# The two first groups of a decoder kernel: from lockstep to leader and follower

## The chip, the cores and the metric

The kernel runs on one core of a Trainium2 chip. A core has five engines that work side by side, each through its own list of instructions in order: PE (TensorE, matmuls and transposes, with PEld for its weight loads), ACT (ScalarE), DVE (VectorE), POOL (GpSimd), and SP (SyncE), which here only issues DMA transfers. They wait for each other through semaphores. The metric is the device time of one execution in microseconds (us); smaller is better. Everything is float32.

## The reference, cut to what matters

There are 32 sequences of 56 tokens with 128 features, and for each sequence a memory of 1500 rows by 128. Two layers follow each other, each with a mixer, a cross attention to the memory and a mixture of experts, and a layer norm after each of the six parts:

```python
x = _layernorm(x + _L0_attn_ref(x, ...))        # 16 heads of 8, window of 32
x = _layernorm(x + _L0_xattn_ref(ctx, ctx, x))  # 1 head of 128, 1500 keys
x = _layernorm(x + _L0_ffn_ref(x, ...))         # 8 experts, 128 -> 512 -> 128, top 2
x = _layernorm(x + _L1_attn_ref(x, ...))        # a gated recurrence along the tokens
x = _layernorm(x + _L1_xattn_ref(x, ctx, ...))  # 16 heads of 64, 1500 keys
x = _layernorm(x + _L1_ffn_ref(x, ...))         # 8 routed experts and a shared one
```

The recurrence is `state = dt * state + (1 - dt) * xt` for 32 state features, with `dt` and `xt` from linear maps of a short convolution; its output is mixed by a gate with another linear map. All experts of both mixtures are computed for all tokens, and weighted.

## The kernel before, in words

The 32 sequences are worked on in 8 groups of 4 (224 tokens, two tiles of 112). A group goes through three stages: *pre* (self attention, first cross attention, first experts, recurrence, and the queries of the second cross attention), *attention* (the second cross attention, which is more than half of the work), and *post* (its projection and the second experts).

Each stage is a Python generator. A `yield` marks a place where the program may put instructions of another generator; a number that is yielded says for how many us of TensorE work the generator should rest, and `None` says that it can't go on yet. There is no other scheduling on the chip: what the generators emit in turn is the order of each engine's list.

In the steady part the generator `attention()` leads, and at each of its yields the loop at the end of the kernel lets `pre(g + 1)` and the `post`s do steps, by a plan in us of TensorE work (`PRE_US`, `share`, `due`). When the attention comes to group g, `pres[g].drain` makes sure that its queries are there.

Before the attention can begin, the queries of group 0 must exist, and there is no attention to hide their computation beside. This opening is the part that the change touches. It computes groups 0 and 1 together, since two groups fill each other's waits. The second group's tiles lie *aside*: in memory that the attention uses later (`s512`, `s384`, `qo[2]` and `m`; the class `Aside`), so that no attention can begin before the second group has left it. Its PSUM banks are those of the attention (`p_s`, three) instead of `p_f` (two). Its first loads of the memory go to `amN`, those of the leader to `cxN`. In the trace a tile of the second group has the name of what it lies in: `s`, `qo`, `m`.

The opening before has three parts, which follow each other:

- `opening_a(0)` and `opening_a(1)`: load, self attention and first cross attention, step by step in turn by `together`. `folding` (a one-time product of the weights of the second cross attention, which needs the 2 MB transfer `heads1`) joins after 10 rounds.
- `opening_b`: `experts_0([first[0], first[1]])` does the experts of both groups in one generator. A weight tile is loaded once and used for both. For expert e it emits the up products and Gelu of group 0, then of group 1, then the down products of expert e-1 for both.
- `opening_c(0)` and `opening_c(1)`: the recurrence of both in turn, and the queries of group 0. `pre(1)`, later, only does the queries of group 1.

The memory is read in loads of 750 KB (`load_x0` for the first cross attention, two sequences at a time; `load_attended` for the second), written back transposed (`memT`), and read again by `load_attended_T` (`amT`). All of them are issued by SP in the order of its list. The first matmul of the attention is the first one that reads `amT`.

The lines of the profile: all matmuls are emitted by the helper at line 142 and transposes at line 151, so their tiles tell them apart. Line 481 is `load_x0`, 1050 `load_attended`, 1053 `load_attended_T`, 507 the store of `memT`, 642 and 644 the experts' weights, 681 the Gelu, 705 the sum over experts, 1165 the load of `heads1`, 319 an affine on ACT, 744 the tanh of the recurrence, 809 the copy of the queries.

Of the kernel before, what the change touches and what calls it, by code (L numbers as in the profile page):

```python
# [9 lines left out]
F32 = mybir.dt.float32  # L10
AF = mybir.ActivationFunctionType
# [53 lines left out]
def decoder_kernel(  # L65
# [241 lines left out]
    def hidden_tile():  # L307
        return mid.tile([P, U0 // D, T], F32, tag="hT", name="hT", bufs=2)
# [271 lines left out]
    def top2(lg):  # L580
        nj = lg.shape[1]

        def col(tag):
            return tiny.tile([TP, nj], F32, tag=tag, name=tag, bufs=2)

        def all_(tag):
            return tiny.tile([TP, nj, E], F32, tag=tag, name=tag, bufs=2)

        def wide_of(c):
            return c.unsqueeze(2).to_broadcast([TP, nj, E])  # L590

        picks = []
        for n in range(2):
            m = col(f"m{n}")
            nc.vector.tensor_reduce(m, lg, AX.X, ALU.max)
            eq = all_("eq")
            nc.vector.tensor_tensor(eq, lg, wide_of(m), ALU.is_equal)
            nc.vector.scalar_tensor_tensor(eq, eq, -float(E), eid_far[:, :nj], ALU.mult, ALU.add)
            first = col("first")
            nc.vector.tensor_reduce(first, eq, AX.X, ALU.min)  # L600
            hot = all_(f"hot{n}")
            nc.vector.tensor_tensor(hot, eid[:, :nj], wide_of(first), ALU.is_equal)
            if n == 0:
# [15 lines left out]
    def router(xT, c0, nj=NJ):  # L619
        ps = bank(p_f, "f")  # L620
        for j in range(nj):
            mm(ps[:TP, j * E : (j + 1) * E], pair(xT, j), sq[:, c0 : c0 + E])
        return ps[:TP, : nj * E].rearrange("p (j e) -> p j e", j=nj)
# [9 lines left out]
        return ps[:TP, :D]  # L633


    def experts_0(groups):

        nu = U0 // D

        def weights(e):  # L640
            wu = wst.tile([P, U0], F32, tag="w0", name="wu0", bufs=4)
            nc.sync.dma_start(wu, wup0[:, e * U0 : (e + 1) * U0])
            wd = wst.tile([P, U0], F32, tag="w0", name="wd0", bufs=4)
            nc.sync.dma_start(wd, wdn0[:, e * U0 : (e + 1) * U0])
            return wu, wd

        def each():
            for k in range(len(groups)):
                place["aside"] = aside if k else None
                yield k  # L650
            place["aside"] = None

        ws = weights(0)
        xT, w, acc, hT = {}, {}, {}, {}
        for k in each():
            xT[k] = to_features(groups[k], "xT")
        yield HOP
        for k in each():
            lg = tiny.tile([TP, NJ, E], F32, tag="lg", name="lg", bufs=2)
            nc.vector.tensor_copy(lg, router(xT[k], C_R0))  # L660
            picks = top2(lg)
            p1 = tiny.tile([TP, NJ], F32, tag="p1", name="p1", bufs=2)
            p2 = tiny.tile([TP, NJ], F32, tag="p2", name="p2", bufs=2)
            nc.vector.tensor_tensor(p2, picks[1][0], picks[0][0], ALU.subtract)
            nc.scalar.activation(p2, p2, AF.Exp)
            nc.vector.tensor_scalar_add(p1, p2, 1.0)
            nc.vector.reciprocal(p1, p1)
            nc.vector.tensor_tensor(p2, p2, p1, ALU.mult)
            w[k] = mix(picks, (p1, p2))
        yield 0  # L670
        for e in range(E + 1):
            last = (ws, dict(hT))
            if e < E:
                if e > 0:
                    ws = nxt
                if e + 1 < E:
                    nxt = weights(e + 1)
                for k in each():
                    hT[k] = hidden_tile()
                    for u in range(nu):  # L680
                        nc.scalar.activation(  # L681
                            hT[k][:, u, :],
                            linear(ws[0][:, u * D : (u + 1) * D], xT[k], T), AF.Gelu,
                            bias=vec[:, C_BUP + e * nu + u : C_BUP + e * nu + u + 1],
                        )
                        if len(groups) == 1:
                            yield 0
                yield 0
            for k in each():
                if e == 0:  # L690

                    wT = work.tile([E, T], F32, tag="wT", name="wT", bufs=1)
                    ps = bank(p_f, "f")
                    for j in range(NJ):
                        mm(pair(ps[:E], j), w[k][:, j, :], ident[:TP, :TP])
                    nc.vector.tensor_copy(wT, ps[:E, :T])
                    if len(groups) == 1:
                        yield HOP
                    acc[k] = [
                        plus(linear(pair(wT, j), bdn, D, TP), groups[k][j], "acc")  # L700
                        for j in range(NJ)
                    ]
                else:
                    for j in range(NJ):
                        nc.vector.scalar_tensor_tensor(  # L705
                            acc[k][j], down(last[1][k], last[0][1], nu, j),
                            w[k][:, j, e - 1 : e], acc[k][j], ALU.mult, ALU.add,
                        )
                        if len(groups) == 1:
                            yield 0  # L710
        both = []
        for k in each():
            both.append([normalize_twice(a, "y") for a in acc[k]])
        yield NORM
        return both


    def recurrent_mixer(both):
        hp = here(hp0, "hp")
        res, hs = [], [h for _, h in both]  # L720
        for t, _ in both:
            r = tok_tile("res")
            nc.vector.scalar_tensor_tensor(r, t, 2.0, rowb("bout1"), ALU.mult, ALU.add)
            res.append(r)
        affine(
            hp[:, :, 1 : S + 1], transposed(hs).rearrange("p (b s) -> p b s", b=G),
            vcol("lnb1"), vcol("lng1"),
# [176 lines left out]

    xin = {}

    def pre(g):
        if g == 1:
            yield from queries_1(query_input(both.pop(1), 1), 1)
            return  # L910
        xs = xin.pop(g) if g in xin else load_x(g)
        if g + 1 < NG:
            xin[g + 1] = load_x(g + 1)
        xs = yield from self_attention(xs)
        xs = yield from cross_attention_0(xs, g)
        (xs,) = yield from experts_0([xs])
        xs = yield from recurrent_mixer(xs)
        xT = query_input(xs, g)
        yield HOP
        yield from queries_1(xT, g)  # L920


    first, both = {}, {}

    def opening_a(g):
        xs = load_x(g)
        load_x0(0, g)
        yield 0
        xs = yield from self_attention(xs)
        first[g] = yield from cross_attention_0(xs, g)  # L930

    def opening_b():
        both[0], both[1] = yield from experts_0([first[0], first[1]])

    def opening_c(g):
        both[g] = yield from recurrent_mixer(both[g])
        if g == 0:
            xT = query_input(both.pop(0), 0)
            yield HOP
            yield from queries_1(xT, 0)  # L940

    attended = set()

# [193 lines left out]
                        if not o.over:  # L1137
                            o.step()

    def together(*threads, lag=0):  # L1140

        n = 0
        while not all(t.over for t in threads):
            for t in threads[:-1] if n < lag else threads:
                if not t.over:
                    t.step()
            n += 1

    flat = sbig.tile([P, CK, 512], F32, tag="s512", name="s512")
    flat = flat.rearrange("p c n -> p (c n)")  # L1150
    room = sbig.tile([P, CK, 384], F32, tag="s384", name="s384")
# [7 lines left out]
    ], folding)  # L1159
    for lo, hi in ((4 * D, 8 * D), (8 * D, N_SQ)):  # L1160
        nc.sync.dma_start(sq[:, lo:hi], sq_w[:, lo:hi])
    starts = [Thread(opening_a(0)), Thread(opening_a(1), aside)]
    for t in starts:
        t.step()
    nc.sync.dma_start(hw, heads1)
    nc.sync.dma_start(w_sh, shared1)
    place["aside"] = aside
    for t, tag in ((qpad0, "qpad"), (hp0, "hp")):
        nc.gpsimd.memset(here(t, tag), 0.0)
    place["aside"] = None  # L1170
    together(*starts, folding, lag=10)
    load_attended_T(0)
    together(Thread(opening_b()))
    together(Thread(opening_c(0)), Thread(opening_c(1), aside))
    pres = [Thread(pre(g)) for g in range(NG)]
    posts = [Thread(post(g)) for g in range(NG)]
    pres[0].over = True
# [121 lines left out]
```

## Time and profile before

| what | us |
|---|---|
| median of three runs | 2385.94 (2383.0 to 2386.28) |
| the profiled execution, its time | 2383.31 |
| the profiled execution, its span | 2381.6 |
| start of the first attention matmul (PE, `s<-qo,amT`) | 276.35 |
| PE busy from 0 to 276 | 202.2, at a mean granted clock of 0.80 |
| PE busy from 276 to 2381 | 2044.9 of 2105, at 0.99 |
| DVE, ACT, POOL busy, share of the span | 60%, 53%, 11% |
| DMA | 163.81 MB, mean 69 GB/s |

The profile is of one execution. Busy time is the time in which an engine has an instruction running; the granted clock is the share of full speed at which TensorE was let run, and a matmul at 0.50 takes about twice as long. A row of the timeline gives the start and length of a run of like instructions, the idle time of the engine before it in square brackets, and what ended that idle time.

### The profile page before, as it was taken

The numbers are of one execution on the slowest core, as the hardware profiler recorded it, in microseconds if no ns is written. First come the engines' busy times: TensorE is split into PE (matmuls) and PEld (weight loads), VectorE is DVE, ScalarE is ACT, GpSimd is POOL, SyncE is SP. The second block draws the span as 40 slices with busy tenths as digits, with TensorE's granted clock in tenths as the row PEclk, the third lists the DMA queues.
The fourth block names the chain that finished last, engine by engine and source line by source line (L and its number), as shares of the span: only waits on it lengthen the run. The fifth ranks groups of instructions, "written<-read, shape, count | busy, mean of one in ns | idle before, by whom it ended". The sixth has DMA issues, their size and how long they took to land. (4 is left out here: it accounts for less than half of the span.)

```text
span 2381.6 us, 37426 instructions
## 1 busy us (share of the span) xinstructions
PE 2247.1 (94%) x14906; PEld 1769.6 (74%) x14906; DVE 1427.0 (60%) x2755; ACT 1262.7 (53%) x2212; POOL 254.3 (11%) x416
## 2 busy tenths in 40 slices
PE   6769799999999999999999999999999999999997
PEld 4548477767876779767887787777787678878787
DVE  3422566766576664766557665666647665566664
ACT  1324365555655456555565556554655555655542
POOL 3100200110021000220003100220002200020000
PEclk8878899999999999999999999999999999999998
DMA  5233010114320233113221133201331022210212
GB/s 157 79 113 91 11 40 26 29 54 122 93 66 16 66 102 108 47 29 108 85 82 37 53 103 94 72 27 59 111 97 58 27 91 62 71 42 28 80 34 82
DMA packets 158159, 163.81 MB, mean 69 GB/s; under 512 B 7417, under 2 KB 134817, under 8 KB 157857
## 3 DMA queue, kind: packets, MB, share of 16 engines
q1 hardware_dynamic: 157984, 161.42, 22.1%
q8 instruction: 118, 1.93, 0.3%
q14 instruction: 57, 0.46, 0.1%
HBM read 135.90 MB, written 25.49 MB: 68 GB/s over the span
## 5 line engine op out<-in xcount | busy, mean ns | idle before, releaser
L142 PE MATMUL v<-amN,s 125*128 125x129 f32 x5376 | 701.3, 276 | 1.8 <-ACT s L1086 1.8
L142 PEld LDWEIGHTS v<-amN,s 125*128 125x128 f32 x5376 | 663.2, 192 | 45.9 <-issue 29.7
L142 PE MATMUL s<-qo,amT 128*125 128x512 f32 (+1 forms) x1536 | 651.5, 547 | 4.7 <-ACT s L998 4.4
L998 ACT COPY s<-s 125x512 f32<-125x512 f32 (+1 forms) x768 | 396.6, 538 | 188.2 <-PE s L142 186.9
L1083 DVE TENSOR_TENSOR s<-s,nb 125x1536 f32<-125x1536 f32 (+1 forms) x256 | 394.3, 1557 | 108.9 <-ACT nb L1075 108.8
L142 PEld LDWEIGHTS s<-qo,amT 128*125 128x125 f32 x1536 | 264.0, 188 | 190.5 <-issue 114.9
L1086 ACT ACTIVATE s<-s 125x1536 f32<-125x1536 f32 (+1 forms) x256 | 337.6, 1327 | 91.3 <-DVE s L1083 87.1
L1001 DVE TENSOR_TENSOR m<-m,s 125x1024 f32<-125x1024 f32 (+1 forms) x256 | 279.0, 1090 | 70.4 <-ACT s L998 65.7
L342 POOL TENSOR_SCALAR rs<-mv 112x1 f32<-112x1 f32 x116 | 46.0, 396 | 1797.9 <-DVE mv L336 1598.8
L1103 ACT ACTIVATE ao<-v,rz 128x128 f32<-128x128 f32 x224 | 80.2, 361 | 176.7 <-DVE rz L1101 174.3
L681 ACT ACTIVATE hT<-f,vec 128x224 f32<-128x224 f32 x224 | 95.3, 449 | 96.8 <-PE f L142 95.1
L142 PE MATMUL f<-xT,wu 128*128 128x224 f32 x448 | 124.2, 381 | 2.8 <-DMA wu<-in_wup_dram 2.0
L142 PE MATMUL f<-pxT,w 128*128 128x224 f32 (+1 forms) x576 | 118.2, 343 | 2.1 <-DMA w<-in_gate_dram 1.3
L1001 DVE TENSOR_TENSOR m<-s 125x1024 f32<-125x1024 f32 x64 | 69.7, 1090 | 83.5 <-ACT s L998 83.2
L142 PEld LDWEIGHTS f<-wd,hT 128*112 128x112 f32 x896 | 104.7, 178 | 13.4 <-ACT hT L681 5.1
L705 DVE SCALAR_TENSOR_TENSOR acc<-f,wmix,acc 112x128 f32<-112x128 f32 x112 | 39.2, 350 | 125.8 <-PE f L142 125.8
L142 PE MATMUL f<-wd,hT 128*112 128x128 f32 x896 | 113.3, 275 | 0.0
L1075 ACT COPY nb<-t 125x512 f32<-125x512 f32 x64 | 34.0, 532 | 148.3 <-PE t L142 148.1
L142 PEld LDWEIGHTS f<-pxT,w 128*128 128x128 f32 x576 | 99.4, 195 | 15.3 <-issue 3.2
L142 PEld LDWEIGHTS f<-xT,wu 128*128 128x128 f32 x448 | 74.0, 194 | 21.2 <-ACT hT L681 7.4
L142 PEld LDWEIGHTS f<-w,h 128*112 128x112 f32 x512 | 67.6, 178 | 24.0 <-issue 9.2
L142 PE MATMUL f<-w,h 128*112 128x128 f32 x512 | 79.7, 279 | 2.0 <-DVE th L870 1.9
(313 smaller groups left out, 2694.2 us busy)
## 6 DMA issues: line engine op xcount, KB each, us to landing
amN<-in_mem_dram SPq DMA_DIRECT2D x36, 750.0 KB
amT<-memT SPq DMA_DIRECT2D x32, 750.0 KB, 4.4
cxN<-in_mem_dram SPq DMA_DIRECT2D x28, 750.0 KB
memT<-big SPq DMA_DIRECT2D x28, 750.0 KB, 5.0
wu<-in_wup_dram SPq DMA_DIRECT2D x56, 256.0 KB, 2.8
wd<-in_wdn_dram SPq DMA_DIRECT2D x56, 256.0 KB, 2.7
w<-in_gate_dram SPq DMA_DIRECT2D x72, 128.0 KB, 2.3
w<-in_up_dram SPq DMA_DIRECT2D x72, 128.0 KB, 2.5
```

The lines of the kernel that those rows point to most:

```text
L142: nc.tensor.matmul(ps, lhsT=lhsT, rhs=rhs, start=start, stop=stop)
L342: nc.gpsimd.tensor_scalar(rs, mv[:, 1:2], mul, add, ALU.mult, ALU.add)
L681: nc.scalar.activation(hT[k][:, u, :], linear(ws[0][:, u * D : (u + 1) * D], xT[k], T), AF.Gelu, bias=vec[:, C_BUP + e * nu + u : C_BUP + ...
L705: nc.vector.scalar_tensor_tensor(acc[k][j], down(last[1][k], last[0][1], nu, j), w[k][:, j, e - 1 : e], acc[k][j], ALU.mult, ALU.add,)
L998: nc.scalar.copy(s[:, c, :], ps[:PK, :n])
L1001: nc.vector.tensor_tensor(m, a, s[:, c - 1 : c + 1, :], ALU.max)
L1075: nc.scalar.copy(nb, ps[:PK, :n])
L1083: nc.vector.tensor_tensor(c, c, nb.unsqueeze(1).to_broadcast([PK, 3, n]), ALU.add)
L1086: nc.scalar.activation(c, c, AF.Exp)
L1103: nc.scalar.activation(o, po[:, :D], AF.Copy, scale=rz)
```

## The change

The opening becomes two generators, `leader` and `follower`, instead of three parts. The leader takes group 0 through everything up to its queries. The follower takes group 1 through the first two stages with a delay of 24 rounds, waits until the leader has emitted its experts (`early["weights"]`), and then does its own experts, with its own loads of all weights. When the leader is over, the follower's sums (`acc`) are copied by POOL out of the aside memory. The rest of group 1, its double normalization, its recurrence and its queries, moves into `pre(1)`, beside the attention of group 0. `experts_0` is a generator for one group again and returns `acc`; the normalization goes to `behind_experts`. The load of `heads1` is issued after the leader's first loads, ahead of the follower's.

```diff
-    def experts_0(groups):
+    def experts_0(xs):
...
-        for k in each():
-            both.append([normalize_twice(a, "y") for a in acc[k]])
-        yield NORM
-        return both
+        return acc
...
     def recurrent_mixer(both):
...
             res.append(r)
+        yield NORM
         affine(
...
+    def behind_experts(acc, g):
+        xs = yield from recurrent_mixer([normalize_twice(a, "y") for a in acc])
+        xT = query_input(xs, g)
+        yield HOP
+        yield from queries_1(xT, g)
+
     def pre(g):
         if g == 1:
-            yield from queries_1(query_input(both.pop(1), 1), 1)
+            yield from behind_experts(early.pop("acc"), 1)
             return
...
-        (xs,) = yield from experts_0([xs])
-        xs = yield from recurrent_mixer(xs)
-        xT = query_input(xs, g)
-        yield HOP
-        yield from queries_1(xT, g)
...
+        acc = yield from experts_0(xs)
+        yield NORM
+        yield from behind_experts(acc, g)
...
-    def opening_a(g):
+    def opening(g):
         xs = load_x(g)
         load_x0(0, g)
         yield 0
         xs = yield from self_attention(xs)
-        first[g] = yield from cross_attention_0(xs, g)
-
-    def opening_b():
-        both[0], both[1] = yield from experts_0([first[0], first[1]])
-
-    def opening_c(g):
-        both[g] = yield from recurrent_mixer(both[g])
+        xs = yield from cross_attention_0(xs, g)
         if g == 0:
-            xT = query_input(both.pop(0), 0)
-            yield HOP
-            yield from queries_1(xT, 0)
+            acc = yield from experts_0(xs)
+            early["weights"] = True
+            yield from behind_experts(acc, g)
+            return
+        while "weights" not in early:
+            yield None
+        acc = yield from experts_0(xs)
+
+        while not leader.over:
+            yield None
+        place["aside"] = None
+        early["acc"] = []
+        for a in acc:
+            t = tok_tile("acc")
+            nc.gpsimd.tensor_copy(t, a)
+            early["acc"].append(t)
...
-    starts = [Thread(opening_a(0)), Thread(opening_a(1), aside)]
-    for t in starts:
-        t.step()
+    leader, follower = Thread(opening(0)), Thread(opening(1), aside)
+    leader.step()
     nc.sync.dma_start(hw, heads1)
     nc.sync.dma_start(w_sh, shared1)
...
-    together(*starts, folding, lag=10)
+    n = 0
+    while not (leader.over and follower.over):
+        for t, at in ((leader, 0), (folding, 10), (follower, 24)):
+            if n >= at and not t.over:
+                t.step()
+        n += 1
     load_attended_T(0)
-    together(Thread(opening_b()))
-    together(Thread(opening_c(0)), Thread(opening_c(1), aside))
```

More of the change, by code (lines that the diff above doesn't have):

```diff
@@ L645, in weights @@
             return wu, wd
[L647 to L651, printed above, removed]
         ws = weights(0)
-        xT, w, acc, hT = {}, {}, {}, {}
-        for k in each():
-            xT[k] = to_features(groups[k], "xT")
+        xT = to_features(xs, "xT")
         yield HOP
[L658 to L669, printed above, removed]
+        lg = tiny.tile([TP, NJ, E], F32, tag="lg", name="lg", bufs=2)
+        nc.vector.tensor_copy(lg, router(xT, C_R0))
+        picks = top2(lg)
+        p1 = tiny.tile([TP, NJ], F32, tag="p1", name="p1", bufs=2)
+        p2 = tiny.tile([TP, NJ], F32, tag="p2", name="p2", bufs=2)
+        nc.vector.tensor_tensor(p2, picks[1][0], picks[0][0], ALU.subtract)
+        nc.scalar.activation(p2, p2, AF.Exp)
+        nc.vector.tensor_scalar_add(p1, p2, 1.0)
+        nc.vector.reciprocal(p1, p1)
+        nc.vector.tensor_tensor(p2, p2, p1, ALU.mult)
+        w = mix(picks, (p1, p2))
         yield 0
+        acc = []
+        hT = None
         for e in range(E + 1):
-            last = (ws, dict(hT))
+            last = (ws, hT)
             if e < E:
@@ L677, in experts_0 @@
                     nxt = weights(e + 1)
[L678 to L697, printed above, removed]
-                        yield HOP
[L699 to L710, printed above, removed]
@@ L711, in experts_0 @@
-        both = []
-        for k in each():
-            both.append([normalize_twice(a, "y") for a in acc[k]])
-        yield NORM
-        return both
+                hT = hidden_tile()
+                for u in range(nu):
+                    nc.scalar.activation(
+                        hT[:, u, :], linear(ws[0][:, u * D : (u + 1) * D], xT, T), AF.Gelu,
+                        bias=vec[:, C_BUP + e * nu + u : C_BUP + e * nu + u + 1],
+                    )
+                    yield 0
+            if e == 0:
+                wT = work.tile([E, T], F32, tag="wT", name="wT", bufs=1)
+                ps = bank(p_f, "f")
+                for j in range(NJ):
+                    mm(pair(ps[:E], j), w[:, j, :], ident[:TP, :TP])
+                nc.vector.tensor_copy(wT, ps[:E, :T])
+                yield HOP
+                for j in range(NJ):
+                    acc.append(plus(linear(pair(wT, j), bdn, D, TP), xs[j], "acc"))
+            else:
+                for j in range(NJ):
+                    nc.vector.scalar_tensor_tensor(
+                        acc[j], down(last[1], last[0][1], nu, j),
+                        w[:, j, e - 1 : e], acc[j], ALU.mult, ALU.add,
+                    )
+                    yield 0
@@ L905, in decoder_kernel @@
     xin = {}
+    def behind_experts(acc, g):
+        xs = yield from recurrent_mixer([normalize_twice(a, "y") for a in acc])
+        xT = query_input(xs, g)
+        yield HOP
+        yield from queries_1(xT, g)
     def pre(g):
         if g == 1:
-            yield from queries_1(query_input(both.pop(1), 1), 1)
+            yield from behind_experts(early.pop("acc"), 1)
             return
@@ L915, in pre @@
         xs = yield from cross_attention_0(xs, g)
-        (xs,) = yield from experts_0([xs])
-        xs = yield from recurrent_mixer(xs)
-        xT = query_input(xs, g)
-        yield HOP
-        yield from queries_1(xT, g)
-    first, both = {}, {}
-    def opening_a(g):
+        acc = yield from experts_0(xs)
+        yield NORM
+        yield from behind_experts(acc, g)
+    early = {}
+    def opening(g):
         xs = load_x(g)
@@ L929, in opening_a @@
         xs = yield from self_attention(xs)
-        first[g] = yield from cross_attention_0(xs, g)
-    def opening_b():
-        both[0], both[1] = yield from experts_0([first[0], first[1]])
-    def opening_c(g):
-        both[g] = yield from recurrent_mixer(both[g])
-        if g == 0:
-            xT = query_input(both.pop(0), 0)
-            yield HOP
-            yield from queries_1(xT, 0)
+        xs = yield from cross_attention_0(xs, g)
+        if g == 0:
+            acc = yield from experts_0(xs)
[13 more added lines that the diff above has]
+            early["acc"].append(t)
     attended = set()
@@ L1138, in drain @@
                             o.step()
[L1140 to L1145, printed above, removed]
-                    t.step()
-            n += 1
     flat = sbig.tile([P, CK, 512], F32, tag="s512", name="s512")
@@ L1161, in decoder_kernel @@
         nc.sync.dma_start(sq[:, lo:hi], sq_w[:, lo:hi])
-    starts = [Thread(opening_a(0)), Thread(opening_a(1), aside)]
-    for t in starts:
-        t.step()
+    leader, follower = Thread(opening(0)), Thread(opening(1), aside)
+    leader.step()
     nc.sync.dma_start(hw, heads1)
```

## The prediction

> **What bounds the kernel now.** I read the table of windows first, then the timelines of PE and SP over the first 300 us. Windows (length, busy us of PE, PEld, DVE, ACT and POOL with instruction counts, granted clock, DMA share, GB/s):
>
> ```profile
> 0.00:59.00 59.00, 38.98 (x246) 25.70 (x246) 19.35 (x35) 11.41 (x22) 18.54 (x49) 0.83 0.53 159
> 112.00:148.00 36.00, 17.51 (x70) 10.84 (x67) 3.84 (x8) 5.46 (x10) 0.00 (x0) 0.62 0.47 148
> 200.00:243.00 43.00, 43.00 (x319) 41.54 (x319) 9.74 (x29) 18.76 (x48) 1.13 (x4) 1.00 0.24 75
> 243.00:276.00 33.00, 17.57 (x64) 11.48 (x63) 19.34 (x69) 7.21 (x17) 13.48 (x35) 0.69 0.03 8
> 276.00:440.00 164.00, 161.22 (x929) 121.38 (x928) 105.76 (x126) 100.67 (x169) 0.00 (x0) 1.00 0.11 34
> 276.00:2381.00 2105.00, 2044.94 (x13577) 1614.21 (x13575) 1330.31 (x2479) 1177.73 (x2034) 206.19 (x302) 0.99 0.21 65
> ```
>
> From 276 on PE is busy 97% of the time: work added there costs its PE time. Before 276 PE is busy 202 of 276 us: only there can waits be saved. The waits are at 0 to 59 (loads), 112 to 148 (loads of the memory) and 243 to 276 (chains through DVE and POOL). The joint experts, 200 to 243, have none.
>
> PE's timeline (start, length, idle before, releaser):
>
> ```profile
> 45.85 2.07 PE L142 MATMUL v<-s 64*128 64x128 f32 x8 [3.05 <-DMA s<-in_heads_dram]
> ...
> 86.82 1.25 PE L151 MATMUL f<-ident,cxN 125*128 125x125 f32 x5
> ...
> 119.88 2.88 PE L151 MATMUL f<-ident,cxN 125*128 125x125 f32 x12 [6.53 <-DMA cxN<-in_mem_dram]
> 127.73 2.89 PE L151 MATMUL f<-ident,cxN 125*128 125x125 f32 x12 [4.97 <-DMA cxN<-in_mem_dram]
> ...
> 143.68 2.73 PE L151 MATMUL s<-ident,amN 125*128 125x125 f32 x12 [3.42 <-DMA amN<-in_mem_dram]
> ...
> 199.79 0.99 PE L142 MATMUL f<-xT,wu 128*128 128x224 f32 x4 [2.01 <-DMA wu<-in_wup_dram]
> ...
> 269.39 7.13 PE L142 MATMUL f<-xT,m 128*128 128x224 f32 x24 [0.63 <-ACT xT L319]
> 276.35 1.02 PE L142 MATMUL s<-qo,amT 128*125 128x512 f32 x2
> ```
>
> SP's timeline:
>
> ```profile
> 20.57 7.87 SPq L481 DMA_DIRECT2D amN<-in_mem_dram  x2
> 28.48 8.00 SPq L1165 DMA_DIRECT2D s<-in_heads_dram  x1
> ...
> 109.53 7.02 SPq L481 DMA_DIRECT2D cxN<-in_mem_dram  x2
> 116.64 15.40 SPq L481 DMA_DIRECT2D amN<-in_mem_dram  x2
> ...
> 163.50 6.81 SPq L481 DMA_DIRECT2D cxN<-in_mem_dram  x2
> 170.41 16.28 SPq L1050 DMA_DIRECT2D amN<-in_mem_dram  x2
> ```
>
> Memory loads follow each other at 8 us each (119.88, 127.73, 143.68 for the first, second and fourth of those issued from 109.53). What SP lists behind a pair waits 16 us for it.
>
> **The change, part by part.** The sum goes from event to event, by the changed program's own lists for PE and SP (an order, no times), with lengths from the rows above.
>
> *Start.* The 2 MB for the folding move ahead of the follower's two loads: 16 us earlier, so they land at 45.85 - 16 = 30. The leader reaches its first folding matmul at about 22 (its scores start at 12.48 and 15.03, then four rounds of DVE, POOL and ACT at 0.6, 0.93 and 0.58 us), so PE waits 8 us there. From the folding to the first transposes of `cxN` took 86.82 - 45.85 = 41 us with two groups. One group with the same folding: bounds 27 (two thirds) and 41; I take 32, nearer the lower end since the second group's half of the DVE, POOL and PE work is gone but the folding stays. Event: 62.
>
> *Leader's first pair.* From 86.82 to the end of its values at 109.4 are 22.6 us, beside the follower's like work. Now the follower's self attention lies beside it, on the same engines: 23. Event: 85. The second pair's loads take 127.73 - 109.53 = 18: 103. The follower's rest of self attention, some 6 us of PE, fills part of it.
>
> *Leader's second pair* from its last landing to its values took 163.4 - 143.68 = 19.7; with the follower's 24 transposes in the list 20.5. Event: 123.5.
>
> *The follower's second pair.* SP now lists the leader's loads for group 2 (two) ahead of these two. Four loads took 143.68 - 109.53 = 34: they land at 157.5. PE has the leader's first expert before that, and then its list blocks: the transposes of `amN` stand ahead of the next experts' matmuls. I count some 17 us lost here. From there to the follower's values the list holds, besides the cross attention that took 19.7, eight up and eight down pairs of the leader's experts; about 24 (bounds 20 and 28). Event: 181.5.
>
> *Two attention loads* come next on SP, ahead of the up weights of the leader's sixth expert. Four loads before them took 199.79 - 163.5 = 36; two take 20: 201.5. PE's list has about 10 us of work until then, so 10 more are lost.
>
> *Leader's last three experts.* One expert for both groups takes 213.12 - 206.49 = 6.63 us at full clock (starts of the up rows), 3.31 for one group; at clock 0.5 twice that. Alone, with two PSUM banks, an up product waits for the Gelu (449 ns each): I take 4.2, the first at half clock, plus the last down products (1.9): 17 (bounds 12 and 21). Event: 218.5.
>
> *Leader's tail.* From the experts' end (243.2) to the first query matmul (269.39) are 26 us with two groups in turn on DVE and POOL. One group, with the follower's experts between its steps: 19 (bounds 14 and 26). Queries: from 269.39 to 278.9 less two attention matmuls of 0.85 each makes 7.8; with the follower's up and down products between, 10.5. Event: 248.
>
> *Follower's end.* The lists leave it four up and five and a half down products of experts: 4.3 experts at 3.65 (three banks) and a last down of 1.75, about 17 (bounds 14 and 28, the latter at half clock). The attention starts at **266**.
>
> Before, it starts at 276.35 with 1.7 us of queries still to come, so 278 in effect: 12 us gained.
>
> *Beside the attention.* The recurrence of group 1 leaves the opening. Its ten PE rows at 252.03 to 261.9 hold 9 us for two groups, partly at half clock; about 3 for one at full clock, transposes included. PE idles 2.8 of 164 us there. Bounds 0 (it fits in that idle time) and 9 (its whole stretch in the opening); I take 3, as the list lets other work stand between. The two POOL copies of 112x128: POOL's like row (`res`) has 0.43 us each; POOL is idle in that stretch. If they stood on the path, 1 us.
>
> *Edits with no price of their own.* Sixteen more weight loads of 256 KB: they land in 2.8 us, while DMA share is 0.24 in the expert stretch; each is issued about one expert (3.65 us) ahead of its use, and an expert shorter than about 3.2 would wait for it. Four more table loads on ACT before the attention (1.28 each in ACT's row); PE has matmuls beside two, the pair before the follower's second exponentials is in the 24 above. One `NORM` rest more for groups 2 to 7 adds no instruction; those threads run beside a PE that is 97% busy, so between -2 and +2.
>
> *Sum:* 2383.3 (the profiled execution) - 12 + 3 = 2374.3. That execution stands 2.6 under the median of the three runs, so **2377**.
>
> **A rule against the trace.** The rows are PE's windows:
>
> ```profile
> 184.20:187.60 3.40, 3.40 (x12) 2.15 (x10) 0.96 (x3) 0.69 (x2) 0.00 (x0) 0.50 0.36 96
> 187.60:191.00 3.40, 3.40 (x11) 2.83 (x11) 0.58 (x2) 1.14 (x3) 0.00 (x0) 0.50 0.37 96
> 191.00:194.40 3.40, 3.40 (x13) 3.12 (x12) 0.00 (x0) 2.00 (x5) 0.00 (x0) 0.50 0.37 96
> 194.40:197.80 3.40, 3.38 (x29) 3.17 (x28) 1.05 (x3) 0.00 (x0) 0.00 (x0) 0.95 0.75 185
> ```
>
> PE is busy without a gap and stays at half clock for 10 us. The Trainium skill ("TensorE: Matmul & The Clock Gate", Part 1: The HAM clock gate) says that one busy window of about 3.4 us lifts the throttle, and that an idle window brings it back. By that rule each of the change's four long waits (at 22, 95, 140 and 192) would cost some 1.7 us of slow matmuls, an estimate from the page, and the sum would be 2370. By the row each costs about 5, as the events above have it. Either way the rule speaks against the change: it adds waits in which PE goes cold and breaks up the one stretch at full clock.
>
> **Rivals.**
> - *The staggering hides more.* If the follower's work fills the waits at 95, 140 and 192 (20 us of the 35 counted), the attention starts at 256: 2367. For it: 202 of 276 us is all the PE work there is. Against: the lists are in order, and the blocking transposes stand ahead of the experts.
> - *Slower: half clock from 201 to the end of the opening.* The leader's three experts cost 6.6 instead of 4.2 (+5 with the first already so), the follower's 4.3 experts +12.5, the tail +3: the attention starts at 286, 2397. For it: 174 to 195 and 246 to 273 were mostly at 0.50 with the same kinds of work. Against: 195 to 246 stayed at full clock. It decides the sign when the opening loses 9 us, that is when the attention starts after 275.
> - *Nothing left.* The opening gains 8, and the recurrence with its stretched chain costs 8 beside the attention: 2386.
>
> **How the numbers follow.** Measurement tells a change from none at about 0.2%, 4.8 us. The forecast's case (the start between 258 and 270) is 2369 to 2381 and has 0.45; the hidden waits 0.13; nothing left (2381 to 2391) 0.19; slower 0.23. Faster is 0.13 and 0.43 of the forecast's 0.45: 0.56; the same 0.2 and slower 0.24. The range leaves out 0.1 on either side: 2363 (start at 252) to 2398 (the half clock rival).
>
> **What would show it.** First `s<-qo,amT` matmul near 266. PE waiting at 22 for `s<-in_heads_dram`, at 140 to 157 for `amN`, at 192 to 201 for `wu`. 64 loads each of `wu` and `wd`. From the first attention matmul to group 2's first transposes (446.94 - 276.35 = 170.6 now) about 3 us more. Wrong would be: a first attention matmul after 275, a granted clock near 0.5 from 200 on, or over 6 us added to that distance.

## The result

The changed kernel takes 2389.29 us, the kernel before 2384.21 (medians of 15 runs each); the ratio is 1.0024, with a 95% interval of 1.0016 to 1.0033. It is slower by a quarter of a per cent, where 2377 and a gain were forecast. The profiled execution after has a span of 2387.8 us, 6.2 more than that of before.

The windows of the changed kernel, with the columns of the prediction's table of windows:

```profile
0.00:59.00 59.00, 42.80 (x265) 30.40 (x266) 19.65 (x36) 11.71 (x22) 18.50 (x48) 1.00 0.55 159
112.00:148.00 36.00, 22.36 (x182) 15.00 (x182) 13.67 (x46) 16.44 (x28) 1.48 (x4) 0.87 0.34 107
185.00:200.00 15.00, 2.38 (x21) 2.29 (x21) 3.50 (x17) 0.45 (x1) 0.05 (x1) 0.76 0.54 138
200.00:243.00 43.00, 35.09 (x178) 26.73 (x179) 15.02 (x53) 16.92 (x36) 6.68 (x18) 0.82 0.24 74
243.00:276.00 33.00, 32.84 (x183) 25.99 (x182) 11.98 (x32) 15.12 (x36) 3.50 (x10) 0.98 0.29 92
276.00:2387.00 2111.00, 2044.80 (x13566) 1617.11 (x13564) 1330.18 (x2496) 1171.55 (x2028) 192.97 (x314) 0.99 0.21 65
```

The stretch from 243 to 276, half idle before, is full now, and a hole stands at 185 to 200.

The clock of 1.00 in the first row is not a measurement of full clock. The clock records of this execution begin at 56.4 us (of the one before: at 30.9), and the view counts the time ahead of the first record as full. The length of like matmuls shows that TensorE was slow there. The last 40 matmuls of the folding, in the changed kernel and then in e1_no_rest, a later run whose lists are the same up to the attention (shortest, median and longest in ns, then the first and last start):

```profile
L142 PE MATMUL v<-s x40: 417/417/579, 37.6 to 51.9; 64*128 64x128 f32 x40
```

```profile
L142 PE MATMUL v<-s x40: 272/272/432, 37.6 to 46.4; 64*128 64x128 f32 x40
```

In the kernel before, the same matmuls take 417 ns at a recorded clock of 0.50 and 272 ns at 1.00. So this execution ran at half clock up to 56.4, where e1_no_rest was at full clock from 37.8 on. For the same reason the clocks given so far for the windows of the kernel before that start at 0 (0.80 and 0.83) are too high.

PE's timeline shows the events of the forecast one by one:

```profile
29.58 4.92 PE L142 MATMUL v<-s 64*128 64x128 f32 x24 [5.72 <-DMA s<-in_heads_dram]
...
67.29 1.04 PE L151 MATMUL f<-ident,cxN 125*128 125x125 f32 x4
...
105.12 1.90 PE L151 MATMUL f<-ident,cxN 125*128 125x125 f32 x8 [4.58 <-DMA cxN<-in_mem_dram]
...
148.90 1.09 PE L151 MATMUL s<-ident,amN 125*128 125x125 f32 x4 [13.39 <-DMA amN<-in_mem_dram]
...
157.09 0.65 PE L151 MATMUL s<-ident,amN 125*128 125x125 f32 x2 [4.25 <-DMA amN<-in_mem_dram]
...
201.14 3.54 PE L142 MATMUL f<-xT,wu 128*128 128x224 f32 x8 [13.28 <-DMA wu<-in_wup_dram]
...
242.57 2.45 PE L142 MATMUL f<-xT,m 128*128 128x224 f32 x8
...
267.94 8.75 PE L142 MATMUL s<-qo,amT 128*125 128x512 f32 x20
```

(In the changed kernel's lines, 641 and 643 load the experts' weights, 1041 is `load_attended`, and 345 is the last step of a normalization, on DVE.)

The attention starts at 267.94, for which 266 were forecast. So the opening did gain, and the loss is behind it. The start of the first attention matmul of each fourth sequence cuts the trace into groups:

| | opening | group 0 | groups 1 to 6 |
|---|---|---|---|
| before | 278.0 | 167.2 | 1683.9 |
| after | 267.9 | 175.4 | 1691.8 |
| difference | -10.1 | +8.2 | +8.0 |

(For the kernel before, the 1.7 us of queries that stand behind its first two attention matmuls are counted as opening; its first attention matmul starts at 276.35.) The differences, taken before rounding, add up to +6.1. Group 7 and the end are alike in both.

Group 0, the kernel before and then the kernel after (busy us of PE, PEld, DVE, ACT and POOL, then the granted clock):

```profile
278.00:445.20 167.20, 164.42 (x967) 125.08 (x966) 109.93 (x131) 103.41 (x171) 0.00 (x0) 1.00 0.11 33
```

```profile
267.90:443.40 175.50, 170.46 (x985) 127.52 (x984) 117.55 (x162) 105.37 (x175) 9.79 (x22) 0.99 0.11 34
```

PE is 6.0 us longer busy and 2.3 us longer idle (5.0 for 2.8). One window of half clock of 3.4 us, at 302, is new there; it can account for 1.7 of the 6.0. That leaves some 4.3 of work, an estimate.

The last 20 us before group 2's attention, before and then after:

```profile
706.70:726.70 20.00, 19.34 (x132) 17.51 (x131) 13.81 (x26) 11.04 (x23) 1.56 (x2) 1.00 0.12 39
```

```profile
707.70:727.70 20.00, 18.43 (x115) 18.12 (x116) 11.34 (x24) 8.86 (x17) 3.67 (x7) 0.83 0.03 12
```

and PE's waits in that place after, for the normalized rows of the next group's queries:

```profile
705.82 0.32 PE L151 MATMUL f<-ident,h 112*128 112x112 f32 x1 [0.53 <-DVE h L345]
...
709.27 0.45 PE L151 MATMUL f<-ident,h 112*128 112x112 f32 x1 [2.22 <-DVE h L345]
```

The same two transposes stood at 698.75 and 700.44 before, 28 and 26 us ahead of the next group's attention; now they stand 22 and 18 us ahead. The windows before groups 3, 5, 6 and 7 are alike: PE 17.8 of 20 us at a clock of 0.91, against 19.3 at 1.00. Before group 4 PE is busy for 17.3 us at full clock, so the idle time comes without a window of half clock too. What the change does to the pre stage of groups 2 to 7 is one more `NORM`, a rest of 6 us of TensorE work, between the experts' sums and the double normalization; besides, it drops some empty yields in the experts and moves the `NORM` that was there behind the next step.

A sentence ahead of the prediction has to be corrected. It says that what the generators emit in turn is the order of each engine's list. That is not so everywhere. SP issues the tokens of groups 2 and 3 (`xin`, four loads) at 39 us before and at 45 us after, though the generators emit them long after the opening's first steps; some step behind the generators draws instructions forward. The prediction itself went by the lists after that step.

### The profile page after: what moved, and what is told of

Read it like the earlier page. It is cut to its first block, busy times and chain, and to the rows that moved or that the text cites. A ratio compares the mean times of both kernels' runs of the same rounds, so it can differ in the third digit from the quotient of the medians.

```text
span 2387.8 us, 37452 instructions
## 1 busy us (share of the span) xinstructions
PE 2251.3 (94%) x14906; PEld 1766.2 (74%) x14906; DVE 1425.9 (60%) x2755; ACT 1267.3 (53%) x2216; POOL 236.8 (10%) x418
## 5 line engine op out<-in xcount | busy, mean ns | idle before, releaser
L342 POOL TENSOR_SCALAR rs<-mv 112x1 f32<-112x1 f32 x124 | 35.4, 286 | 1646.4 <-DVE mv L336 1490.2
L142 PE MATMUL f<-xT,wu 128*128 128x224 f32 x448 | 125.6, 382 | 14.2 <-DMA wu<-in_wup_dram 13.3
```

The source lines that it names most:

```text
L142: nc.tensor.matmul(ps, lhsT=lhsT, rhs=rhs, start=start, stop=stop)
L342: nc.gpsimd.tensor_scalar(rs, mv[:, 1:2], mul, add, ALU.mult, ALU.add)
```

## The experiments

All ratios are to runs of the kernel before on the same chip. Stretches are of one profiled execution each. *Fourth sequences* is the sum, over groups 1 to 6, of the last sequence's stretch, in which the next group's queries are finished; it varies least between executions.

| kernel | opening | group 0 | groups 1 to 6 | fourth sequences | median | ratio (95%) |
|---|---|---|---|---|---|---|
| before | 278.0 | 167.2 | 1683.9 | 342.5 | 2384.21 | 1 |
| changed | 267.9 | 175.4 | 1691.8 | 351.3 | 2389.29 | 1.0024 (1.0016 to 1.0033) |
| e1_no_rest | 262.7 | 175.5 | 1683.6 | 344.1 | 2379.26 | 0.9999 (0.9987 to 1.001) |
| e2_before_rest | 277.5 | 167.2 | 1684.9 | 349.1 | 2388.53 | 1.0032 (1.0021 to 1.0043) |
| e3_rec_in_opening | 281.3 | 169.9 | 1687.0 | 351.8 | 2393.11 | 1.006 (1.0048 to 1.0072) |
| e5_rec_alone | 272.1 | 175.0 | 1688.0 | 344.3 | 2385.55 | 1.0021 (1.0013 to 1.003) |
| e6_late_load | 258.9 | 175.6 | 1686.1 | 344.5 | 2372.74 | 0.9959 (0.9943 to 0.9975) |
| e7_later_rec | 266.4 | 173.9 | 1681.6 | 344.3 | 2374.4 | 0.9961 (0.9948 to 0.9975) |
| e8_all | 252.0 | 180.2 | 1679.6 | 344.1 | 2364.99 | 0.9927 (0.9912 to 0.9942) |
| e9_loads_apart | 248.7 | 174.0 | 1678.9 | 343.0 | 2359.47 | 0.9923 (0.9906 to 0.9939) |
| e10_rest_early | 266.2 | 176.7 | 1719.8 | 338.5 | 2416.66 | 1.0161 (1.0142 to 1.018) |

(For before, e2_before_rest and e5_rec_alone the opening includes the 1.7 us of queries behind the first attention matmuls.)

The openings differ by some us also where nothing in them was changed, and this difference arises early: with the same lists, the changed kernel has its second pair of memory loads at 105.1 and e1_no_rest at 98.6. From this second landing (the second wait for `cxN`) to the start of the attention it is 162.8 us in the changed kernel, 164.1 in e1_no_rest, 163.0 in e7_later_rec and e10_rest_early, 159.0 in e6_late_load, 148.6 in e8_all and 148.1 in e9_loads_apart. For what a change does to the rest of the opening these distances are the better measure.

### The rest, taken out and put in

```diff
         acc = yield from experts_0(xs)
-        yield NORM
         yield from behind_experts(acc, g)
```

> The changed kernel without the added rest between the experts' sums and the double normalization of groups 2 to 7 (one line); nothing else. Theory (the rest makes each group's queries late, and the last steps before the next group stand with too little attention beside them): the stretches of groups 1 to 6 fall back by 8 us in all to those of the kernel before (281.2, 283.2, 279.1, 280.7, 279.1, 280.6), the total to about 2381, ratio to the kernel before 0.9985 to 0.999. Rival (the longer groups come from the other order of tiles and loads that the change leaves behind, not from the rest): the stretches stay at 284.0, 283.4, 281.8, 282.3, 280.4, 280.0 and the total at 2389. Group 0 stays at 175 in both.

The stretches of groups 1 to 6 fall from 1691.8 to 1683.6, which is what the kernel before has, and group 0 stays at 175.5. The ratio falls from 1.0024 to 0.9999. The 0.999 that was expected at most was not reached, though its interval holds it: without the rest the change is neither faster nor slower, as far as can be measured. (The profiled execution is the fastest of its eleven, 5 us under their median, so its stretches are a low measure, the opening's 262.7 above all.) The same stretch before group 2, in this kernel:

```profile
699.30:719.30 20.00, 19.58 (x135) 17.81 (x134) 13.99 (x26) 11.28 (x24) 1.32 (x2) 1.00 0.12 39
```

The other way round, the rest alone in the kernel before:

```diff
         # experts_0, ahead of the normalization
+        if len(groups) == 1:
+            yield NORM
         both = []
```

> The kernel before with only this rest put in, at the same place, for groups 2 to 7. Theory of the rest: the fourth sequence of each group takes 1 to 2.6 us longer, 8 us in all, ratio 1.003; a window of half clock appears near the end of most groups. Rival (order of tiles and loads): no change, ratio 1.000.

The median is 8 us above the kernel before, 1.0032, as expected, and the fourth sequences take 349.1 for 342.5. In the profiled execution, the second fastest of its six, other sequences were shorter, so that the sum over groups 1 to 6 shows only 1.0 us of it: these sums move by some us from one execution to the next. The place looks like that of the changed kernel:

```profile
707.10:727.10 20.00, 17.77 (x121) 17.22 (x121) 12.60 (x28) 8.92 (x17) 4.95 (x8) 0.91 0.08 33
```

So the rest costs about 8 us by itself here, and taking it out of the changed kernel gave 6 by the ratios. Is it that the last steps come late, or the rest at any place?

```diff
-            work_.append((pres[group + 1], PRE_US, p / 0.88))
+            work_.append((pres[group + 1], PRE_US, p / 0.82))
```

> The changed kernel with its rest kept, but the plan for the pre stage ends earlier (due by p / 0.82 instead of p / 0.88). Theory (the rest costs only because it makes the last steps late, with too little attention left beside them): the last 20 us of each group are as before (PE 19.3 busy, full clock), the fourth sequences at 57 to 58, groups 1 to 6 sum to 1684, total 2381, ratio 1.000. Rival (a rest between sums and normalization costs by itself, at whatever place): 1690 or more in all, total 2389, ratio 1.002 to 1.003.

Half of the theory holds: with the whole pre stage drawn forward the fourth sequences take 338.5, less than in the kernel before, and the last 20 us are full, at full clock:

```profile
707.70:727.70 20.00, 19.40 (x114) 16.43 (x115) 14.66 (x25) 11.36 (x23) 5.36 (x3) 1.00 0.20 61
```

The total was missed by far. The earlier steps now crowd the other sequences (the second one of a group takes 71 to 74.5 for 67 to 68), and groups 1 to 6 take 28 us more. So the hole at the group's end goes when the steps come earlier, which fits lateness. But the edit moves the whole pre stage, not the rest alone, and leaves less of it to the fourth sequences; that the price of the rest is lateness and nothing else is not shown by it. The total of the rival, 1690 or more, isn't ruled out either. The plan's 0.88 is not free to move.

### The recurrence, in the opening or beside the attention

The changed kernel with group 1's normalization and recurrence in the follower's part of the opening:

```diff
         acc = yield from experts_0(xs)
-        while not leader.over:
-            yield None
-        ...
+        early["both"] = yield from recurrent_mixer([normalize_twice(a, "y") for a in acc])
```

> The changed kernel, rest kept, with group 1's normalization and recurrence put back into the follower's part of the opening; beside the attention only its queries stay. Theory (the recurrence costs 7 to 8 us beside the first attention, more than the 3 forecast, through waits and half clock in its first sequences): group 0's stretch falls from 175.4 to 167 to 169, the first attention matmul comes later by the follower's own chain, 15 to 20 us (it stands alone at the end), so the total is 8 to 13 us above the changed kernel, 2397 to 2402. Rival (group 0 is longer because the attention starts with the follower's leftovers, not because of the recurrence): group 0 stays at 173 to 175, total 2404 to 2410.

Group 0 falls to 169.9, so 5.5 of its 8.2 us go with the recurrence and its normalization, and the rival's 173 is not what came; the other 2.7 us are not accounted for. The start moves from 267.9 to 281.3, since the chain stands alone at the end of the opening, and the ratio is 1.006, 8.6 us above the changed kernel: as expected. In the staggered opening the recurrence is therefore better beside the attention. PE's waits at the end of that opening (in this kernel, 715 and 757 are steps of the recurrence on DVE):

```profile
269.67 0.32 PE L151 MATMUL s<-ident,s 112*128 112x112 f32 x1 [1.68 <-DVE s L345]
272.24 0.45 PE L151 MATMUL s<-ident,s 112*128 112x112 f32 x1 [2.25 <-DVE s L345]
274.72 3.79 PE L142 MATMUL s<-qo,sq 128*32 128x224 f32 x10 [2.03 <-DVE qo L715]
...
280.80 0.66 PE L142 MATMUL s<-sq,qo 128*112 128x128 f32 x4 [1.63 <-DVE qo L757]
```

The same move alone, in the kernel before, with its lockstep:

```diff
-        both = []
-        for k in each():
-            both.append([normalize_twice(a, "y") for a in acc[k]])
+        both = [[normalize_twice(a, "y") for a in acc[0]]]
+        ...                      # acc[1] is copied out by POOL
...
+            pair_ = [normalize_twice(a, "y") for a in both.pop(1)]
+            yield NORM
+            xs = yield from recurrent_mixer(pair_)
...
-    together(Thread(opening_c(0)), Thread(opening_c(1), aside))
+    together(Thread(opening_c(0)))
```

> The kernel before, in lockstep, with only one part of the change: group 1's sums are copied out by POOL and its normalization, recurrence and queries go beside the attention of group 0. Theory: the opening loses the second thread of the last chains, 276 to about 269; group 0 gains 6 to 8 us as in the changed kernel; total within 3 us of the kernel before. Rival (PE price alone, 3 us): group 0 at 172, total 4 us below the kernel before, 2380.

The first attention matmul comes at 270.4 instead of 276.35; with the queries behind it the opening falls from 278.0 to 272.1, and group 0 rises from 167.2 to 175.0. The ratio is 1.0021: a loss of some 5 us, more than the 3 us that the theory allowed, and far from the rival's gain. In lockstep the second thread in the last chains cost 5.9 us, and the same work beside the attention 7.8. The other 4 us of this execution, the slowest of its eleven, lie in groups 1 to 6, where nothing was changed.

Is it the place, the first blocks, in which the products with the values do not run yet?

```diff
         if g == 1:
+            yield 45.0
             yield from behind_experts(early.pop("acc"), 1)
```

> The changed kernel without the rest, and with group 1's normalization, recurrence and queries held back by 45 us of TensorE work, past the first sequence of the attention. Theory (the recurrence is dear because it falls into the first blocks, where the matmuls on the values do not yet run and little stands beside it): group 0's stretch falls from 175.5 to 171 to 172, total 2375, ratio 0.998. Rival (its chain costs the same at any place beside the attention): the 7 us move from the first sequence to the second, stretch 175, total 2379.

The first sequence takes 26.8 us instead of 33.9, but the third 57.4 instead of 50.8; group 0 falls by 1.6 only. The rival is nearer: the chain takes 6 to 7 us at either place. The theory of the place falls for most of the price. The ratio is 0.9961, 9 us below e1_no_rest's (6 us by the medians, each against the kernel before on its own chip), of which the profiled stretches of the two show 1.6 in group 0 and 2.0 in groups 1 to 6; since the profiled execution of e1_no_rest lies 5 us under its median, little of that is settled.

### The waits of the opening

The two waits of 13 us, at 135 and at 187, were forecast from SP's list. SP's timeline of the changed kernel:

```profile
87.07 6.71 SPq L481 DMA_DIRECT2D cxN<-in_mem_dram  x2
...
122.90 6.66 SPq L481 DMA_DIRECT2D cxN<-in_mem_dram  x2
133.95 11.06 SPq L481 DMA_DIRECT2D amN<-in_mem_dram  x2
...
178.61 0.79 SPq L1041 DMA_DIRECT2D amN<-in_mem_dram  x1
...
186.02 0.78 SPq L1041 DMA_DIRECT2D amN<-in_mem_dram  x1
186.90 8.63 SPq L641 DMA_DIRECT2D wu<-in_wup_dram  x1
```

The two `cxN` loads at 122.90 are for group 2, needed some 300 us later. They were held back by a data dependence, a small POOL write into the tile that reads the follower's sums, behind the opening:

```diff
-            elif max(g + 1, 2) < NG:
-                load_x0(0, max(g + 1, 2))
+            elif g and g + 1 < NG:
+                load_x0(0, g + 1)
...
+    for i in range(2):
+        nc.gpsimd.tensor_copy(cxN[i][:1, 0, :1], early["acc"][1][:1, :1])
+    load_x0(0, 2)
     load_attended_T(0)
```

> The changed kernel without the rest, and the leader's loads of the memory for group 2 made to wait for the end of the follower's experts (a small POOL write into the tile that reads them), so that they no longer stand ahead of the follower's second pair and of the weights. Theory (the two waits of 13 us in the opening are the queue of 8 us loads): the follower's second pair lands 16 us earlier, the first attention matmul comes at 248 to 252 instead of 263 to 268, total 2365, ratio to the kernel before 0.993 to 0.995. Rival (PE finds no work for that time, or the half clock takes it): start at 260 or later, total 2376 or more.

The ratio is 0.9959, 9.5 us better than e1_no_rest's, but the start is 258.9, where 248 to 252 were expected. The first wait falls from 13.4 to 9.0 us only, because the follower's own loads, which can't start before its first pair is done (at 128.6 here, at 134.0 in the changed kernel), still take 16; the second stays:

```profile
139.13 1.10 PE L151 MATMUL s<-ident,amN 125*128 125x125 f32 x4 [8.97 <-DMA amN<-in_mem_dram]
...
192.07 3.55 PE L142 MATMUL f<-xT,wu 128*128 128x224 f32 x8 [13.48 <-DMA wu<-in_wup_dram]
```

So the two loads for group 2 held up the opening by 4 to 5 us, which is also what the distances from the second landing show (159.0 for 162.8 to 164.1). The rest of the 9.5 lies elsewhere and is not settled by one profiled execution of each.

With e7's rest of 45 us added, and the load for the second attention sequence held back in the same way:

```diff
+    nc.gpsimd.tensor_copy(amN[1][:1, 0, :1], early["acc"][1][:1, :1])
```

> Both of the former, and the load of the second attention sequence also held back behind the follower's experts. Theory: start of the attention at 240 to 245, since the weights of the leader's sixth expert then wait for one load of 8 us instead of two; group 0's stretch 171 to 172; total 2354 to 2358, ratio 0.989 to 0.991. Rival (loads that are held back collide with the first loads of the attention): group 0's stretch over 176, total 2362 or more.

The second wait falls from 13.5 to 5.0 us, the distance from the second landing to the start from 159.0 to 148.6, and the ratio is 0.9927. The start is 252.0 where 240 to 245 were expected. The rival's collision is there too: the three loads that are held back now stand ahead of the second load of the transposed memory, and group 0 takes 180.2:

```profile
283.44 2.04 PE L142 MATMUL s<-qo,amT 128*125 128x512 f32 x2 [4.18 <-DMA amT<-memT]
```

So the loads for group 2 were made to wait for group 1's normalized rows instead, inside the stretch of group 0 (the lines that held them back in the opening go, the one for `amN` stays):

```diff
             yield from behind_experts(early.pop("acc"), 1)
+            for i in range(2):
+                nc.gpsimd.tensor_copy(cxN[i][:1, 0, :1], res1[1][1][:1, :1])
+            load_x0(0, 2)
```

> As the last kernel with everything together, but the loads of the memory for group 2 wait for group 1's normalized rows beside the attention (about 395), instead of standing ahead of the second load of the transposed memory at 254. Theory (the 4.2 us wait of PE for that load, the half clock after it and the slower first sequence are the collision): the start stays at 250 to 254, group 0's stretch falls from 180.2 to 173 to 175, total 2359, ratio 0.990. Rival (the first sequence is longer for another reason): group 0 stays near 180, total 2365.

The loads are issued at 327, not at the 395 that was expected. Group 0 is back at 174.0, so the collision was the reason. The start is 248.7; the 3.3 us against e8_all lie ahead of the second landing, and this profiled execution is the fastest of its six. The median is 2359.47, the ratio 0.9923 (0.9906 to 0.9939). This kernel is faster than both: the leader and follower, without the rest, with the 45 us of e7_later_rec and with three loads moved. Its interval overlaps that of e8_all, so the last step by itself is shown in the stretch and not in the ratio.

## Why the prediction was wrong

The likeliest case, and the sign, were wrong; the opening was right nearly event by event. In the profiled executions a gain of 9 us was forecast and a loss of 6.1 measured. Of these 15 us, 1.9 lie in the opening, 5.2 in the recurrence beside the attention, and 8.0 in a term that was put at nothing, the rest.

- *Start to follower's end.* The forecast's events against the measured ones: folding 30 and 29.6, first `cxN` transposes 62 and 67.3, second landing 103 and 105.1, the follower's second pair landed 157.5 and 157.1, the up weights 201.5 and 201.1, first attention matmul 266 and 267.9. The waits of 17 us for `amN` and 10 us for `wu` measured 13.4 + 4.3 and 13.3. The forecast's gain of 12 measured 10.1. Reading the lists of SP and PE against the 8 us of a memory load was enough for that. It is not exact to more than some 5 us, and that it came within 2 is partly luck: the first `cxN` transposes came 5 us late, with half clock up to 56.4, and the leader's first pair, from 67.3 to the issue of the next loads at 87.07, took 19.8 us where 23 were forecast. e1_no_rest has the same lists up to there, was at full clock from 37.8, and starts at 262.7.
- *Beside the attention.* The step was "I take 3, as the list lets other work stand between". It measured 8.2: about 4.3 of PE work, up to 1.7 for a window of half clock and 2.3 of idle PE. The ends of the range, 0 and 9, held it; the value was taken from the wrong end. The row of the kernel before that was nearest, 9 us for the whole stretch of two groups in the opening, was set aside with the words above. e5_rec_alone and e7_later_rec show 7.8 and 6.7 us for it. One of the prediction's own signs of being wrong came with it: from the first attention matmul to group 2's first transposes, at 445.10, it is 177.2 us, 6.6 more than the 170.6 of before.
- *Edits with no price of their own.* This is the step that failed outright: "One `NORM` rest more for groups 2 to 7 adds no instruction; those threads run beside a PE that is 97% busy, so between -2 and +2". It measured 8.0 in the stretches, and e1_no_rest and e2_before_rest give 6 and 8 us of it in the medians, taken out and put in. That the rest costs this much is shown by these two runs; how it does so is read from the traces: a rest adds no work, but it moves the same work towards a due time, the next group's attention (the transposes for its queries stood 22 and 18 us ahead instead of 28 and 26), where less is left to stand beside it. PE was idle 2.2 of the last 20 us instead of 0.7 in most groups, and went to half clock for a window. The plan lets the pre stage end near 0.88 of the group; what stands behind it had not been read in the windows of before.
- *The rival "slower"* named half clock from 201 to the end of the opening. That did not happen: the opening ended at 268, at a clock of 0.82 and 0.98 in the last two windows. The rival "nothing left" had the right size for the second step (8 us beside the attention) and lacked the rest; that its 2386 came nearest to 2389 is partly luck.
- *The rule on the clock.* The Trainium skill ("TensorE: Matmul & The Clock Gate", Part 1: The HAM clock gate) would lift the half clock after one busy window of 3.4 us; the prediction stayed with a row that showed 10 us. After the wait for the weights, half clock held on until 210.0, about 9 us after PE had resumed at 201.14. But PE was not busy all that time, it waited 2.1 us for a Gelu ahead of 206.79. The recorded stretches of half clock in this opening last 3.4, 6.8, 13.7 or 17.1 us, so windows of 3.4 us that end at 210.0 fit them:

```profile
203.10:206.50 3.40, 1.59 (x4) 0.78 (x4) 0.88 (x6) 3.34 (x5) 0.00 (x0) 0.50 0.19 61
206.60:210.00 3.40, 3.21 (x15) 3.21 (x16) 0.35 (x1) 0.47 (x2) 0.00 (x0) 0.50 0.03 11
210.00:213.40 3.40, 3.34 (x19) 2.17 (x19) 0.35 (x1) 1.79 (x4) 0.00 (x0) 1.00 0.25 77
```

  The first window in which PE was nearly always busy is the last one at half clock, which is what the rule gives. So this wait agrees with the page, the prediction's row (10 us without a gap at 0.50) does not, and no run here settles what makes the difference. The prediction's 2370 by the page was also not carried through: four waits at 3.3 us less each would be 13 us, not 7.

## What to carry to other kernels

A rest or a yield in a plan with due times is work moved, not nothing: before it is priced at zero, read the window in front of the due time and ask what is left there to stand beside the moved steps. A chain of small dependent steps beside a full engine costs more than its instructions on that engine; here 7 to 8 us for some 4 of matmuls, at any of the places tried. In an opening that loads set, SP's list and the time of one load forecast the events to some 5 us, and a load that nobody needs yet can be taken out of the way with a data dependence, but whatever it then stands in front of has to be looked up as well.

## What was not expected of the hardware

- Memory loads, in packets of 512 bytes, ran at about 8 us for 750 KB, some 96 GB/s, in the stretches looked at, while the 2 MB of `heads1`, in packets of 16 KB, landed within about 7 us of the end of the loads ahead of it (316 GB/s from 23.0 to 29.6). That the size of the packets is the reason was not tested. The order on SP mattered more than the number of bytes: the 16 extra weight loads of the change (4.2 MB) caused no wait of their own, while the two early loads for group 2 made up 4.4 of the first wait's 13.4 us, and the load for the second attention sequence 8.5 of the second's 13.5.
- The same lists gave starts of the attention between 262.7 (e1_no_rest) and 267.9 (the changed kernel). The difference is there by the second landing (98.6 and 105.1), ahead of which TensorE ran at half clock up to 56.4 in one execution and up to 37.8 in the other; behind it the two differ by 1.3 us.
